# Feed-forward part of a fused convolution and Mamba kernel: the program's order on every engine, a second half put off by a strip, taps in fours

## The chip, the cores and the metric

The kernel runs on one core of one Trainium2 chip. The metric is device time in microseconds (us); the time before is the median of three runs. A profile is one execution recorded by the hardware profiler. TensorE multiplies matrices (PE in the profile, its weight loads PEld), VectorE is DVE, ScalarE is ACT, GpSimd is POOL, and SyncE (SP) issues the transfers.

## The reference, cut to what matters

The input is an image batch of 4 x 64 channels x 128 x 128, float32, and four layers follow one another: a Mamba layer, a mixing layer in a transformed domain, two convolutions with a gate, and a last layer of two convolutions, a Mamba block and a feed-forward block. Only the feed-forward block is touched. With `t` the tokens after the Mamba block:

```
t = t + pvt2ffn(layernorm(t, ln2_w, ln2_b), Hh, Ww, fc1_w, fc1_b, dw_w, dw_b, fc2_w, fc2_b)
y = t.transpose(0, 2, 1).reshape(Bn, C, Hh, Ww)
return x + y

def pvt2ffn(t, Hh, Ww, fc1_w, fc1_b, dw_w, dw_b, fc2_w, fc2_b):
    h = t @ fc1_w.T + fc1_b                       # 64 -> 256 channels
    himg = ...                                    # as an image, 256 x 128 x 128
    himg = conv2d(himg, dw_w, dw_b, groups=Ch)    # 3 x 3, each channel by itself
    h = gelu(himg)                                # back as tokens
    return h @ fc2_w.T + fc2_b                    # 256 -> 64 channels
```

## The kernel before

The kernel is one program of five parts. The last, `layer3_ffn`, reads from device memory the normalised tokens `n3` (`d_n` in the profile) and `s3` (`d_s`), the sum to which its result is added, and writes `out`. It goes through 32 strips: 4 images by 8 strips of R = 16 rows of 128 columns, in a Python loop that is unrolled in full.

The 256 hidden channels are split in two groups of 128. Group 1 (tile `h1`) is convolved on VectorE, group 0 (tile `h0`) on TensorE.

- `first(b, r0, H)` (from line 1409) makes the hidden rows of one strip. It zeroes a border row of the tile `N` at the top strip (L1416) or the bottom strip (L1418) of an image, both on VectorE, loads `N` in two transfers (L1423), and then in six steps, three for `h1` and three for `h0`, multiplies by `f1` into the PSUM tile `ph` (L1436) and lets ScalarE add the bias into `h1` or `h0` (L1441). GpSimd zeroes the border columns (L1427, L1428) and rows (L1430, L1432). It is a generator: the main loop calls it for the strip after, one step after each third tap.
- `taps(h1)` (from line 1454) is VectorE's convolution: one multiplication (L1463) and eight multiply-adds (L1461), each over 16 x 128 elements of 128 channels, into the tile `g1`. It stops after the taps 4 and 8.
- The main loop, for a strip, loads `res` from `s3` in four transfers (L1479). For each half `kk` of the strip (8 rows) it multiplies by nine diagonal matrices, one for each tap, in four 64 x 64 corners of the array, into the PSUM tiles `pd` (L1489), and ScalarE takes the gelu into `g0` (L1499). After the first half comes the gelu of `g1`, in place (L1501).
- Then the first taps of the strip after are called, and after them the output products: for each half `kk`, the PSUM tile `po` gets `f2` times `g1` (L1513) and `f2h` times `g0` (L1516), VectorE adds bias and `res` into `o` (L1520), and after both halves four transfers store `o` (L1524).

`po` and `ph` have one buffer[...], `pd` two buffers[...]. `N`, `h0`, `h1`, `g0`, `g1`, `res` and `o` have two buffers.

The order of the calls is not the order of the instructions: a scheduler of the language takes, for each engine, the instruction that it finds ready and most urgent by its own costs. The two Mamba layers prevent that with a method `pin`, which adds to each new instruction a dependence, without a semaphore, on the one called before it on the same engine. `layer3_ffn` had no such thing.

Of the kernel before, what the change touches and what calls it, by code (L numbers as in the profile page):

```python
# [10 lines left out]
F32 = mybir.dt.float32  # L11
AF = mybir.ActivationFunctionType
ALU = mybir.AluOpType
# [4 lines left out]
P = 128  # L18
B, C, HH, WW = 4, 64, 128, 128
# [94 lines left out]
class _Consts:  # L114


    def __init__(self, nc, pool, cst, upto=None):
        w = _OFF[upto][1] if upto else _CONST.shape[1]
        self.t = pool.tile([P, w], F32, name="cst")
        nc.sync.dma_start(self.t, cst[:, :w])  # L120
# [20 lines left out]

class _Mamba:


# [17 lines left out]
    def __init__(self, ctx, tc, K, nst, w, kinds, bufs, slots={}):  # L164
        nc = self.nc = tc.nc
        self.tc = tc
        self.K, self.nst, self.ng, self.kinds, self.bufs = K, nst, nst // NQ, kinds, bufs
        cp = self.cp = ctx.enter_context(tc.tile_pool(name="mc", bufs=1))
        self.wp = ctx.enter_context(tc.tile_pool(name="mw", bufs=2))
        self.dram = ctx.enter_context(tc.tile_pool(name="md", bufs=2, space=DRAM))  # L170
        self.bp = ctx.enter_context(tc.tile_pool(name="mb", bufs=1, space=PSUM))
        self.misc = ctx.enter_context(tc.tile_pool(name="mm", bufs=1, space=PSUM))
        self.prev, self.seen = {}, None

        self.slots = slots

        wx, xpd, dtw = (self.tmp(k)[:n, :DI] for k, n in (("wx", P), ("xpd", 4), ("dtw", 4)))
        for h in range(2):
            nc.sync.dma_start(wx[64 * h : 64 * (h + 1)], w["in_wT"][:, :DI])
        self.taps = []  # L180
        for k in range(2):
            cw = cp.tile([P, DI], F32, name=f"cw{k}")
            for h in range(2):
                nc.sync.dma_start(
                    cw[64 * h : 64 * (h + 1)],
                    w["conv_wT"][2 * k + h : 2 * k + h + 1, :].to_broadcast([64, DI]),
                )
            nc.vector.tensor_mul(cw, wx, cw)
            self.taps.append(cw)
        self.wz = cp.tile([P, DI], F32, name="wz")  # L190
        nc.vector.memset(self.wz, 0.0)
        nc.sync.dma_start(self.wz[64:], w["in_wT"][:, DI:])
        self.wbc = cp.tile([P, 2 * nst], F32, name="wbc")
        nc.sync.dma_start(self.wbc, w["xp_bcT"])
        self.wC = cp.tile([P, max(nst, DD)], F32, name="wC")
        nc.vector.memset(self.wC, 0.0)
        nc.vector.tensor_copy(self.wC[:, :nst], self.wbc[:, nst:])
        self.spread = {}
        for g in (g for g, kind in enumerate(kinds) if kind == "D"):
            s = self.spread[g] = cp.tile([P, P], F32, name=f"spread{g}")  # L200
            nc.vector.tensor_copy(
                s.rearrange("p (q e) -> p q e", q=NQ),
                self.wbc[:, NQ * g : NQ * (g + 1)].unsqueeze(2).to_broadcast([P, NQ, DD]),
            )

        nc.sync.dma_start(xpd, w["xp_dt"])
        nc.sync.dma_start(dtw, w["dt_wT"])
        pm = self.pm()
        nc.tensor.matmul(pm[:, :DI], xpd, dtw, start=True, stop=True)
        self.wdt = cp.tile([P, DI], F32, name="wdt")  # L210
        nc.vector.tensor_copy(self.wdt, pm[:, :DI])

        cols = {}
        for k in ("conv_b", "dt_b", "D"):
            cols[k] = cp.tile([P, 1], F32, name=f"col_{k}")
            nc.sync.dma_start(cols[k], w[k])
        self.conv_b, self.dt_b, self.z_b = cols["conv_b"], cols["dt_b"], 0.0
        self.dD = cp.tile([P, P], F32, name="dD")
        nc.vector.tensor_scalar(
            self.dD.rearrange("p (j e) -> p j e", j=ND),  # L220
            K.eye.rearrange("p (e j) -> p j e", j=ND),
            cols["D"],
            None,
            ALU.mult,
        )
        self.A = cp.tile([P, ND, self.ng], F32, name="A")
        with nc.allow_non_contiguous_dma(reason="the states on the partitions"):
            for q in range(NQ):
                for j in range(ND):
                    nc.sync.dma_start(  # L230
                        self.A[DD * q : DD * (q + 1), j, :],
                        w["A_log"].rearrange("(e j) (g q) -> j q e g", j=ND, q=NQ)[j, q],
                    )
        nc.scalar.activation(self.A, self.A, AF.Exp)
        nc.vector.tensor_scalar_mul(self.A, self.A, -1.0)
        self.state = cp.tile([P, ND, self.ng], F32, name="state")


        self.ring = cp.tile([P, 2 * ND, GAP + TC], F32, name="ring")
# [28 lines left out]
    def halves(self, *pairs):  # L268
# [5 lines left out]
                for i, (l, r) in enumerate(pairs)  # L274
            )
        )

    def pin(self):

        ins = self.nc.cur_bb.bb.instructions  # L280
        n = len(ins)
        while n and ins[n - 1] is not self.seen:
            n -= 1
        for i in ins[n:]:
            if i.engine in self.prev:
                self.tc.add_manual_dep(
                    i,
                    self.prev[i.engine],
                    mybir.DependencyInfo(mybir.DependencyClass.NoSync, mybir.DependencyReason.DATA),
                    reason="order",  # L290
                )
            self.prev[i.engine] = i.name
        self.seen = ins[-1]

    def t(self, name, bufs=None, w=TC):
        return self.wp.tile([P, w], F32, name=name, tag=name, bufs=bufs)
# [124 lines left out]
    def run(self, chunks, ahead, behind, leads, budget):  # L421
# [3 lines left out]
        nc = self.nc  # L425
# [7 lines left out]
        n = len(its)  # L433
# [15 lines left out]
        owed, full = [], None  # L449
# [65 lines left out]
                    for q in range(NQ):  # L515
                        nc.sync.dma_start(t[DD * q : DD * (q + 1)], rows)

        self.seen = nc.cur_bb.bb.instructions[-1]
        for gen in (ahead, self.prepare):
            for _ in gen(chunks[0]):  # L520
                pass
        replicated(-1)
        produced(0)
        self.pin()
        first, second = {}, {}
        at = -1
        for c in chunks[1:]:
# [4 lines left out]
        for i, (u, j) in enumerate(its):  # L532
# [20 lines left out]
            while nexp < min(n, i + 4) and its[nexp][1] in its[nexp][0]["c"].get("dl", ()):  # L553
                v, k = its[nexp]
# [47 lines left out]
            while owed and not full and (owed[0][0] <= i or i + 1 == n):  # L602
                _, v, h = owed.pop(0)
# [4 lines left out]
                    break  # L608
            beside(i, budget[i % per])
            replicated(i)  # L610
            self.pin()
        for f in list(feeds):
            finished(f)
        finished(started(behind(chunks[-1], self.gated(chunks[-1])), n))
# [747 lines left out]
def layer3_ffn(ctx, tc, K, w, n3, s3, out):  # L1362
# [4 lines left out]
    nc = tc.nc  # L1367
    R = 16
    HR = (R + 2) // 2
    NK = R // 8  # L1370
# [79 lines left out]
    H = {}  # L1450
# [3 lines left out]
    def taps(h1):  # L1454

        g1 = wp.tile([P, R, WW], F32, name="g1", tag="g1")
        for k in range(9):
            dy, dx = divmod(k, 3)
            tap, wk = h1[:, dy : dy + R, dx : dx + WW], dww[:, 1, k : k + 1]
            if k:  # L1460
                nc.vector.scalar_tensor_tensor(g1, tap, wk, g1, ALU.mult, ALU.add)  # L1461
            else:
                nc.vector.tensor_scalar(g1, tap, wk, None, ALU.mult)  # L1463
            if k in (4, 8):
                yield g1

    for g1 in taps(H[1]):
        pass
    for n, (b, r0) in enumerate(strips):
        simg = s3[b].rearrange("c (r w) -> c r w", w=WW)  # L1470
        oimg = out[b].rearrange("c (r w) -> c r w", w=WW)
        h0 = H[0]
        H = {}
        ahead = first(*strips[n + 1], H) if n + 1 < len(strips) else iter(())
# [4 lines left out]
            nc.sync.dma_start(res[half[q % 2], q // 2], simg[:, r0 + 4 * q : r0 + 4 * q + 4, :])  # L1479

        g0 = [wp.tile([P, NK, 4, WW], F32, name=f"g0{i}", tag=f"g0{i}") for i in range(2)]
        for kk in range(NK):
            pd = [dp.tile([P, 4, WW], F32, name=f"pd{i}", tag=f"pd{i}") for i in range(2)]
            for k in range(9):
# [10 lines left out]
                        )  # L1495
                if k % 3 == 2:
                    next(ahead, None)
            for i in range(2):
                nc.scalar.activation(g0[i][:, kk], pd[i], AF.Gelu, bias=dwb[:, i : i + 1])  # L1499
            if not kk:  # L1500
                nc.scalar.activation(g1, g1, AF.Gelu, bias=dwb1)  # L1501
        for _ in ahead:
            pass

        later = taps(H[1]) if H else iter(())
        g2 = next(later, None)

        o = wp.tile([P, NK, 4, WW], F32, name="o3", tag="o3")
        for kk in range(NK):
            po = op.tile([P, 2, 4, WW], F32, name="po", tag="po")  # L1510
            for h in range(2):
                r = 8 * kk + 4 * h
                nc.tensor.matmul(po[half[h], h], f2, g1[:, r : r + 4, :], start=True, stop=False)  # L1513
            for i in range(2):
                for h in range(2):
                    nc.tensor.matmul(  # L1516
                        po[half[h], h], f2h[half[h], i, :], g0[i][half[h], kk], start=False, stop=i == 1
                    )
            for h in range(2):
                nc.vector.scalar_tensor_tensor(  # L1520
                    o[half[h], kk], po[half[h], h], b2[half[h]], res[half[h], kk], ALU.add, ALU.add
                )
        for q in range(R // 4):
            nc.sync.dma_start(oimg[:, r0 + 4 * q : r0 + 4 * q + 4, :], o[half[q % 2], q // 2])  # L1524
        next(later, None)
        g1 = g2


def _col(v):
# [97 lines left out]
```

## Time and profile before

| | |
|---|---|
| median of 3 runs | 19720.83 us (19693.8 to 19727.24) |
| the profiled execution's own time | 19736.35 us |
| its span in the profile | 19734.5 us |
| feed-forward part in it | 18,452 us to the end |
| granted TensorE clock over the span | 0.869 of full speed |

The profile's page gives the busy time of each engine over the whole span and in 40 equal slices; the feed-forward part is a small share of it, so the whole-span shares say little on it. The trace can be asked for windows of time, for the waits in a window (who waited, for whom, total us, times, longest), and for the instructions in order of time. In its lines, `out<-in` names the tiles, `xN` counts instructions run together, and brackets give the idle time before and what ended it. A float32 matrix product shows as two records.

### The profile page before, as it was taken

What the parts mean: (1) busy time and instruction counts of PE and PEld (TensorE: products, weight loads), DVE (VectorE), ACT (ScalarE), POOL (GpSimd) and SP (SyncE); (2) the same over time, 40 slices, a digit from 0 to 9 for tenths busy, and PEclk for the clock granted to TensorE, in tenths of its full rate; (3) what the DMA queues carried; (4) which work ended last, traced back from release to release, by engine and by line L of the source; (5) the groups of instructions that cost most, each with busy time, mean ns of one, the idle gap of its engine ahead of it and who ended that gap; (6) DMA issues with size and microseconds to landing.
All of it is one profiled execution on the core that took longest, in us unless ns stands there. A gap on an engine that the chain in (4) does not pass through costs nothing. (4 is left out here: it accounts for less than half of the span.)

```text
span 19734.5 us, 238606 instructions
## 1 busy us (share of the span) xinstructions
PE 15294.8 (78%) x80186; PEld 7627.5 (39%) x80186; DVE 15836.0 (80%) x8739; ACT 14933.8 (76%) x30369; POOL 14205.9 (72%) x8094
## 2 busy tenths in 40 slices
PE   7778788778897777777777777777777777777777
PEld 3333333367434333333333333333333333333222
DVE  7888888722124999999999999999999999999755
ACT  7888888411324988889888888988889888888422
POOL 6888888500003898899988989998898988989300
PEclk8999899879998888888888888888888888888888
DMA  5555555300212232332323233232322323233111
GB/s 138 152 150 153 154 150 151 95 37 26 75 56 65 75 88 77 84 82 79 87 75 87 78 83 86 76 88 77 83 82 79 87 76 86 78 82 85 46 43 38
DMA packets 669524, 1722.89 MB, mean 87 GB/s; under 512 B 196785, under 2 KB 231937, under 8 KB 660865
## 3 DMA queue, kind: packets, MB, share of 16 engines
q1 hardware_dynamic: 668288, 1707.62, 31.6%
q8 instruction: 629, 10.31, 0.2%
q14 instruction: 607, 4.96, 0.1%
HBM read 1434.27 MB, written 272.63 MB: 86 GB/s over the span
## 5 line engine op out<-in xcount | busy, mean ns | idle before, releaser
L596 POOL TENSOR_TENSOR ring<-ring,cb 128x1024 f32<-128x1024 f32 x5120 | 12086.1, 2378 | 1653.5 <-DVE ring L593 1340.8
L593 DVE TENSOR_TENSOR_SCAN ring<-da,state,bx 128x1024 f32<-128x1024 f32 x4848 | 11143.4, 2335 | 971.1 <-PE bx L494 697.9
L556 ACT ACTIVATE da<-dl,A 128x1024 f32<-128x1024 f32 x5120 | 5868.2, 1146 | 1383.0 <-DVE ring L593 1365.9
L387 ACT ACTIVATE bxT<-duT,BT 128x128 f32<-128x128 f32 x21504 | 6757.2, 387 | 0.0
L494 PE MATMUL bx<-cst,bxT 128*128 128x128 f32 x24576 | 4458.7, 338 | 2842.8 <-DVE bx L587 2053.0
L494 PEld LDWEIGHTS bx<-cst,bxT 128*128 128x128 f32 x24576 | 3743.1, 214 | 4917.0 <-DVE bx L587 2068.7
L413 PE MATMUL y<-ring,cst 128*32 128x512 f32 x20480 | 3566.6, 660 | 332.4 <-POOL ring L596 332.2
L587 DVE TENSOR_TENSOR bx<-du,bx 128x1024 f32<-128x1024 f32 x2048 | 2515.5, 1228 | 339.6 <-PE bx L500 219.1
L413 PEld LDWEIGHTS y<-ring,cst 128*32 128x32 f32 x20480 | 532.3, 112 | 1735.7 <-POOL ring L596 856.1
L1145 PE MATMUL cv<-img,cw 64*64 64x512 f32 x9216 | 1008.2, 594 | 74.6 <-DMA img<-d_x 45.6
L500 PE MATMUL bx<-xc,spread 128*128 128x512 f32 x2048 | 1018.0, 620 | 1.4
L1427 POOL MEMSET h<- 128x18 f32 x64 | 8.3, 132 | 1180.5 <-PE pd L1489 793.5
L1076 POOL TENSOR_TENSOR xs<-xs,cl 128x1024 f32<-128x1024 f32 x32 | 74.9, 2340 | 1068.4 <-DVE cl L1075 1068.4
L391 POOL TENSOR_TENSOR bxT<-duT,BT 128x512 f32<-128x512 f32 x768 | 809.2, 1054 | 11.5 <-ACT duT L370 11.5
L1310 POOL MEMSET X<- 64x1 f32 x4 | 0.4, 89 | 1122.4 <-DMA cw<-in_l_conv_wT 1122.4
L1489 PE MATMUL pd<-h,diag 64*64 64x512 f32 x4608 | 687.9, 610 | 0.7 <-issue 0.7
L1145 PEld LDWEIGHTS cv<-img,cw 64*64 64x64 f32 x9216 | 437.2, 134 | 643.5 <-issue 568.0
L593 DVE TENSOR_TENSOR_SCAN ring<-da,bx 128x1024 f32<-128x1024 f32 x272 | 609.4, 2276 | 72.4 <-PE bx L494 52.8
L500 PEld LDWEIGHTS bx<-xc,spread 128*128 128x128 f32 x2048 | 347.7, 189 | 687.7 <-issue 464.1
L1461 DVE SCALAR_TENSOR_TENSOR g<-h,dww,g 128x2048 f32<-128x2048 f32 x256 | 602.0, 2352 | 11.2
L1441 ACT ACTIVATE h<-ph,ff_fc_b 128x384 f32<-128x384 f32 (+1 forms) x384 | 200.7, 577 | 497.9 <-PE ph L1436 480.1
L1059 ACT COPY O<-p 128x1024 f32<-128x1024 f32 x32 | 32.4, 1012 | 691.7 <-PE p L1052 691.7
(321 smaller groups left out, 13361.0 us busy)
## 6 DMA issues: line engine op xcount, KB each, us to landing
cb<-c SPq DMA_DIRECT2D x5120, 128.0 KB, 2.8
dl<-d SPq DMA_DIRECT2D x2048, 128.0 KB, 3.4
du<-d SPq DMA_DIRECT2D x2048, 128.0 KB, 3.0
d<-pos SPq DMA_DIRECT2D x128, 512.0 KB, 2.6
d<-u SPq DMA_DIRECT2D x128, 512.0 KB, 3.0
X<-d_t SPq DMA_DIRECT2D x124, 256.0 KB, 4.0
S<-in_x SPq DMA_DIRECT2D x120, 256.5 KB, 4.4
res<-in_x SPq DMA_DIRECT2D x128, 128.0 KB, 3.8
```

Source lines behind the costliest of these rows:

```text
L387: nc.scalar.activation(t[:, k, q].rearrange("p e j -> p (e j)"), c["duT"][:, k, :], AF.Copy, scale=c["BT"][:, k, n : n + 1])
L391: nc.gpsimd.tensor_mul(t[:, k].rearrange("p q e j -> p q (e j)"), c["duT"][:, k].unsqueeze(1).to_broadcast(shape), c["BT"][:, k, NQ * g : ...
L413: nc.tensor.matmul(c["y"][DD * j : DD * (j + 1), _COLS[h]], K.sel, hc[:, _COLS[h]], start=False, stop=u["g"] == self.ng - 1,)
L494: nc.tensor.transpose(bx[:, P * k : P * (k + 1)], v["bxT"][:, k, :, :, j].rearrange("p q e -> p (q e)"), self.K.eye)
L500: nc.tensor.matmul(bx[:, k], self.spread[v["g"]], v["c"]["xc"][:, k], start=True, stop=True)
L556: nc.scalar.activation(das[nexp], v["c"]["dl"][k], AF.Exp, scale=self.A[:, k, v["g"] : v["g"] + 1])
L587: nc.vector.tensor_mul(bxs[i], u["c"]["du"][j], u["B"])
L593: nc.vector.tensor_tensor_scan(hs, das.pop(i), bxs.pop(i), 0.0 if u["c"].get("reset") else st, ALU.mult, ALU.add)
L596: nc.gpsimd.tensor_mul(hc, hs, u["cb"])
L1145: nc.tensor.matmul(p[i][half[h]], W[half[i], k, :], src[half[i], at : at + 4, dx : dx + WW], start=k == 0, stop=k == 8,)
L1461: nc.vector.scalar_tensor_tensor(g1, tap, wk, g1, ALU.mult, ALU.add)
L1489: nc.tensor.matmul(pd[i][half[h]], diag[half[i], k, :], h0[half[i], r : r + 4, dx : dx + WW], start=k == 0, stop=k == 8,)
```

## The change

The method `pin` becomes a class of its own, `_Pin`, with the same action; the Mamba layers' loop calls it at the same places. `layer3_ffn` makes one such object before its loop and calls it after each tap and at the end of each half, so that each engine's instructions, the issuing of transfers too, go out in the order of the calls.

The order of the calls changes. The output products of the first half (`kk` = 0) are called in the middle of the second half's taps, after the tap k = 3. Those of the second half are kept in `owed` and called in the next strip, after the tap k = 3 of its first half, with the stores of the strip. VectorE's nine taps are called in three pieces: taps 0 to 3 after the first half and the gelu of `g1`, taps 4 to 7 after the output products of the first half, and tap 8 after the owed half in the next strip. The first strip's nine taps are called ahead of the loop. The last owed half comes after it.

```
+class _Pin:
+    def __init__(self, tc):
+        self.tc, self.prev = tc, {}
+        self.seen = tc.nc.cur_bb.bb.instructions[-1]
+    def __call__(self):
+        ...
...
-            if k in (4, 8):
-                yield g1
+            yield g1
...
+    def more(gen, n):
+        for _ in range(n):
+            g = next(gen, None)
+        return g
+
+    def second(n, g0, g1, res, o, kk):
+        b, r0 = strips[n]
+        po = op.tile([P, 2, 4, WW], F32, name="po", tag="po")
+        ...
+        for h in range(2):
+            nc.vector.scalar_tensor_tensor(
+                o[half[h], kk], po[half[h], h], b2[half[h]], res[half[h], kk], ALU.add, ALU.add
+            )
+        if kk == NK - 1:
+            oimg = out[b].rearrange("c (r w) -> c r w", w=WW)
+            for q in range(R // 4):
+                nc.sync.dma_start(oimg[:, r0 + 4 * q : r0 + 4 * q + 4, :], o[half[q % 2], q // 2])
+
+    pin = _Pin(tc)
+    g1 = more(taps(H[1]), 9)
+    rest, owed = iter(()), None
     for n, (b, r0) in enumerate(strips):
...
         for kk in range(NK):
...
                 if k % 3 == 2:
                     next(ahead, None)
+                if (kk, k) == (0, 3) and owed:
+                    second(*owed)
+                    more(rest, 1)
+                if (kk, k) == (1, 3):
+                    second(n, g0, g1, res, o, 0)
+                    more(rest, 4)
+                pin()
             for i in range(2):
                 nc.scalar.activation(g0[i][:, kk], pd[i], AF.Gelu, bias=dwb[:, i : i + 1])
             if not kk:
                 nc.scalar.activation(g1, g1, AF.Gelu, bias=dwb1)
-        for _ in ahead:
-            pass
-        later = taps(H[1]) if H else iter(())
-        g2 = next(later, None)
...
-        next(later, None)
-        g1 = g2
+                rest = taps(H[1]) if 1 in H else iter(())
+                g2 = more(rest, 4)
+            pin()
+        owed, g1 = (n, g0, g1, res, o, 1), g2
+    second(*owed)
```

More of the change, by code (lines that the diff above doesn't have):

```diff
@@ L138, in _rstd @@
     nc.scalar.activation(out, out, AF.Exp, scale=-0.5)
+class _Pin:
[3 more added lines that the diff above has]
+    def __call__(self):
+        ins = self.tc.nc.cur_bb.bb.instructions
+        n = len(ins)
+        while n and ins[n - 1] is not self.seen:
+            n -= 1
+        for i in ins[n:]:
+            if i.engine in self.prev:
+                self.tc.add_manual_dep(
+                    i,
+                    self.prev[i.engine],
+                    mybir.DependencyInfo(mybir.DependencyClass.NoSync, mybir.DependencyReason.DATA),
+                    reason="order",
+                )
+            self.prev[i.engine] = i.name
+        self.seen = ins[-1]
 class _Mamba:
@@ L172, in __init__ @@
         self.misc = ctx.enter_context(tc.tile_pool(name="mm", bufs=1, space=PSUM))
-        self.prev, self.seen = {}, None
         self.slots = slots
@@ L276, in halves @@
         )
[L278 to L293, printed above, removed]
     def t(self, name, bufs=None, w=TC):
@@ L516, in replicated @@
                         nc.sync.dma_start(t[DD * q : DD * (q + 1)], rows)
-        self.seen = nc.cur_bb.bb.instructions[-1]
+        pin = _Pin(self.tc)
         for gen in (ahead, self.prepare):
@@ L523, in run @@
         produced(0)
-        self.pin()
+        pin()
         first, second = {}, {}
@@ L610, in run @@
             replicated(i)
-            self.pin()
+            pin()
         for f in list(feeds):
@@ L1463, in taps @@
                 nc.vector.tensor_scalar(g1, tap, wk, None, ALU.mult)
-            if k in (4, 8):
-                yield g1
-    for g1 in taps(H[1]):
-        pass
+            yield g1
[7 more added lines that the diff above has]
+        for h in range(2):
+            r = 8 * kk + 4 * h
+            nc.tensor.matmul(po[half[h], h], f2, g1[:, r : r + 4, :], start=True, stop=False)
+        for i in range(2):
+            for h in range(2):
+                nc.tensor.matmul(po[half[h], h], f2h[half[h], i, :], g0[i][half[h], kk], start=False, stop=i == 1)
+        for h in range(2):
+            nc.vector.scalar_tensor_tensor(
+                o[half[h], kk], po[half[h], h], b2[half[h]], res[half[h], kk], ALU.add, ALU.add
+            )
+        if kk == NK - 1:
[5 more added lines that the diff above has]
+    rest, owed = iter(()), None
     for n, (b, r0) in enumerate(strips):
         simg = s3[b].rearrange("c (r w) -> c r w", w=WW)
-        oimg = out[b].rearrange("c (r w) -> c r w", w=WW)
         h0 = H[0]
@@ L1481, in layer3_ffn @@
         g0 = [wp.tile([P, NK, 4, WW], F32, name=f"g0{i}", tag=f"g0{i}") for i in range(2)]
+        o = wp.tile([P, NK, 4, WW], F32, name="o3", tag="o3")
         for kk in range(NK):
@@ L1497, in layer3_ffn @@
                     next(ahead, None)
+                if (kk, k) == (0, 3) and owed:
[4 more added lines that the diff above has]
+                    more(rest, 4)
+                pin()
             for i in range(2):
@@ L1501, in layer3_ffn @@
                 nc.scalar.activation(g1, g1, AF.Gelu, bias=dwb1)
-        for _ in ahead:
-            pass
-        later = taps(H[1]) if H else iter(())
-        g2 = next(later, None)
[L1508 to L1524, printed above, removed]
-        next(later, None)
-        g1 = g2
+                rest = taps(H[1]) if 1 in H else iter(())
+                g2 = more(rest, 4)
+            pin()
+        owed, g1 = (n, g0, g1, res, o, 1), g2
+    second(*owed)
 def _col(v):
```

## The prediction

> **What bounds the kernel now.** I went from the table of busy time by slices (the feed-forward part is the last 2.6 of its 40 slices) to the busy time by windows, the waits of that stage and the timeline of single strips. Everything outside this part keeps its instructions and their order: the pinning moved from a method to a class, and the two Mamba layers call it at the same places. So only the time from 18,452 us to the end is in question.
>
> The windows, columns as named in the second line: two windows, one of about a strip and, for later, one of a convolution stage.
>
> ```profile
> core 0: us, PE busy (x) PEld busy (x) DVE busy (x) ACT busy (x) POOL busy (x), PEclk, DMA share, GB/s
> 5400.00:5700.00 300.00, 300.00 (x2800) 104.72 (x2796) 47.98 (x64) 67.71 (x92) 0.00 (x0) 1.00 0.15 50
> ...
> 19111.40:19151.20 39.80, 30.64 (x192) 9.03 (x192) 23.10 (x13) 10.64 (x17) 0.35 (x4) 0.84 0.16 42
> ```
>
> In 39.8 us TensorE is busy 30.6, VectorE 23.1, ScalarE 10.6: no engine is full. The waits of the stage (18,490 us to the end; total us, times, longest) say why:
>
> ```profile
> DVE g L1463 <- ACT h L1441: 321.9, 31, 10.8
> ...
> ACT g L1501 <- DVE g L1461: 299.9, 30, 10.9
> PE po L1513 <- DVE o L1520: 288.1, 32, 10.1
> ...
> DVE o L1520 <- PE po L1516: 177.5, 33, 16.8
> ```
>
> TensorE loses 9.0 us a strip to VectorE's addition (L1520), and VectorE loses 10.4 to `h` and 5.4 to TensorE: the two stand in each other's way in turn. The timeline (start, duration) shows it in one strip:
>
> ```profile
> 19130.75 1.28 DVE L1463 TENSOR_SCALAR g<-h,dww 128x2048 f32<-128x2048 f32 x1 [10.59 <-ACT h L1441]
> ...
> 19131.83 0.92 PE L1436 MATMUL ph<-N,f 64*128 64x384 f32 x4
> 19132.07 19.13 DVE L1461 SCALAR_TENSOR_TENSOR g<-h,dww,g 128x2048 f32<-128x2048 f32 x8
> ...
> 19135.42 0.92 PE L1436 MATMUL ph<-N,f 64*128 64x384 f32 x4
> ...
> 19139.85 1.08 PE L1513 MATMUL po<-g,f 128*64 128x512 f32 x4
> ...
> 19151.24 1.53 DVE L1520 SCALAR_TENSOR_TENSOR o<-po,fc2b__124169,res 64x512 f32<-64x512 f32 x2
> 19151.30 2.00 ACT L1501 ACTIVATE g<-g,dwb 128x2048 f32<-128x2048 f32 x1 [9.97 <-DVE g L1461]
> ...
> 19152.82 1.97 PE L1513 MATMUL po<-g,f 128*64 128x512 f32 x4 [9.18 <-DVE o L1520]
> ```
>
> All nine taps of the next strip run in one piece, 19,130.75 to 19,151.2. The first half's products are in `po` by 19,143, but the addition that frees the single `po` is queued behind the taps; the second half's products stand at the head of TensorE's queue until 19,152.82. The additions of halves 0 are at 18,522.44 for strip 0 and 19,700.82 for strip 30: 39.28 us a strip.
>
> [...]after the 9.18 us wait the first L1513 group took 1.97 us instead of 1.08. [...]here, with one core, the window at 5,400 us shows 300 of 300 us busy at clock 1.00.[...]
>
> **The change part by part.** I write t for the time in a strip, from its first `pd` product.
>
> *TensorE, the sum.* Three taps of `pd` and one `ph` group come every 3.58 us at full clock (19,131.83 to 19,135.42); six of these are 21.5. One `po` half is 12 matmul records: 1.0 for the four of L1513, four steps of 0.43 for the eight of L1516, 2.75; two are 5.5. Sum 27.0 with no stall. Nothing is added or removed; the order is.[...]
>
> *The path through one strip.* k0-2 0 to 2.6, `ph` to 3.6, k3 to 4.4, owed `po` half to 7.3, then k4-8 with two `ph` groups: kk=0 ends at 13.6. Its gelus are needed late: those of the strip before end by 2.4, `po` wants them at 4.4. ScalarE after kk=0: `h` 13.8 to 14.9 (1.07 after the `ph` start, 1.05 long), two `pd` gelus to 16.15, gelu of `g1` (2.00) to 18.2. TensorE in kk=1: k0-2 and `ph` to 17.15, k3 to 18.0, then `second(n, 0)`, which needs `g1` at 18.2: a new wait, 0.2 to 0.5. I take 0.3: **27.3 us a strip**, from 26.8 (a cheaper `po`, no wait) to 28.5[...]. The half clock goes with the 9 us stall.
>
> *VectorE, in its own order.* Taps 0-3 (1.32 + 3 x 2.39 = 8.5) start when `h1` is complete, 14.9, end 23.4; addition of half 0, whose `po` is ready at 21.1, to 24.9; taps 4-7 (9.6) to 34.5, which is 7.2 of the next strip; addition of the owed half, `po` ready 7.3, to 8.8; tap 8 to 11.2. Behind the additions wait taps 4-7 and tap 8; the gelu of `g1` wants tap 8 at 16.15, so 5 us are spare. Busy 23.4 of 27.3, waiting 3.7: VectorE doesn't bound. `po` is free at 8.8 and 24.9, wanted at 18 and at 31.7.
>
> *Image starts.* `first` issues VectorE's zeroing of the top row of `N` (L1416, 0.17 us) at the strip's start, in program order now behind tap 7, so done at 7.4; the `ph` at t=2.7 of strips 7, 15 and 23 reads that row. TensorE waits 4.7[...]. Three times 6.2 is 18.6 us (0 to 30). The bottom row (L1418) is read only by the third group, at 12.8: hidden. Loads of `N` don't wait for it: they were issued at 18,707.7, the zeroing ran at 18,718.9.
>
> *SP, POOL.* The four stores of a strip (0.47 each to issue) come after the owed addition, at 8.8 to 10.7 of the next strip, past the two loads of `N` and four of `res`, which are now issued ahead of them and, for the strip after, behind them: ten issues, some 5.5 of 27.3 us. `N` for the strip after goes out by 12 and lands 4.3 later, wanted at 30; `res` is wanted at 21 of the next strip. Cost zero; with that slack of 14 us gone, TensorE would wait for `ph`. POOL does four small memsets a strip (0.13 each); their tiles are free half a strip before ScalarE writes them: zero. All tiles that live longer have two buffers. Bytes per strip are the same in less time: 42 x 39.28/27.3 = 60 GB/s, and the page shows slices of 150.
>
> *The sum.* Strip 0 depends on the same chain as now (first `h`, nine taps until 18,497.5); its `pd` ended at 18,510.2, and with one `po` half in between strip 1 starts at 18,512.9. Thirty strips of 27.3 are 819, image starts 18.6. Strip 31 has no `ph`: 15.5 + 2.75 + the wait to 21.4, gelus and the last half to 25, addition 1.53: 26.4; from the last addition to the end 3.2, as now. 18,512.9 + 819 + 18.6 + 29.6 = 19,380, 354 below the span of 19,734.5. The profiled execution took 19,736.35, which gives 19,382; the median of the runs is 15.5 lower, so **19,366**.
>
> **Rivals.** (1) *VectorE becomes the bound*: its order now alternates with TensorE, and if the 5.4 us for `po` of today stay beside 23.4 busy and 1.7 for `h`, a strip is 30.5 us: 30 x 3.2 = 96 more, 19,462. For it: taps 4-7 end within 0.1 us of the owed `po`. Against: each `po` is ready when VectorE comes. Chance 0.11.
>
> (2) *Slower: the array stays at half clock.*[...] 27.0 us of products become 54, 14.7 more than 39.28: 30 x 14.7 = 441, 20,162. It decides below a mean clock of 27.0/39.28 = 0.69. For it: the clock of this stage is 0.84 to 0.89 now[...]. Against: clock 1.00 in the full convolution window. Chance 0.06.
>
> (3) *The change doesn't do what it says*: the order is still that of today, nine taps in front of the addition. Then 19,721. For it: the call order was a wish before as well, and was not kept. Against: the same pinning sets the Mamba layers' order. Chance 0.03.
>
> **How the numbers follow.** The forecast, TensorE-bound at 26.8 to 28.5 us, has 0.80. Its bottom: 15 for 26.8 and 19 for free image starts, with 22 for the scatter of runs (the lowest is 27 below the median): 19,310. Its top: 36 for 28.5 and 11 for the image starts, some 19,415. I widen the range to 19,470 to take in rival 1. What a measurement of this kernel can tell from no change is about 0.2%, 39 us. The first two cases are faster (0.91), the third is the same (0.03), the second rival slower (0.06).
>
> **What would show it.** Right: additions of halves 0 at 27.3 us steps, TensorE's wait for L1520 near nothing, clock near 1.00, VectorE waiting 3 to 4 us before the first tap, a small wait of `po` for the gelu of `g1`, and three longer waits of `ph` at image starts behind L1416. Wrong: a strip over 28.5 us, or a wait of TensorE over 1 us in an ordinary strip; the name of who ends it tells which step failed.

## The result, and the profile after

The changed kernel took 19,395.9 us (median of four runs, 19,381.6 to 19,397.5) against 19,722.3 before: 0.9836 of it, 95% interval 0.9819 to 0.9853, or 326 us less. The forecast was 19,366 within 19,310 to 19,470.

In the two profiled executions the feed-forward part, from the addition into its bias (L1397, now L1403) to the end, took 1270.9 us before (18,463.59 to 19,734.5) and 939.6 us after (18,453.95 to 19,393.5): 331 us less. It began 9.6 us earlier in the second one. The layers ahead are unchanged, but in the ten profiled executions of this document they end anywhere between 18,413 and 18,466 us. That scatter is as large as some of the differences below, so the strip and the time from that addition to the end (the stage time) are compared beside the totals.

The busy time in a window of exactly one strip of the changed kernel:

```profile
core 0: us, PE busy (x) PEld busy (x) DVE busy (x) ACT busy (x) POOL busy (x), PEclk, DMA share, GB/s
18936.60:18964.58 27.98, 27.98 (x194) 8.63 (x193) 23.03 (x14) 10.40 (x17) 0.35 (x4) 1.00 0.25 59
```

A strip takes 27.98 us where it took 39.28. TensorE is shown busy without a gap, at a granted clock of 1.00; before, it was busy 30.6 of 39.8 us at 0.84. The waits of the stage, 18,490 us to the end (who waited for whom: total us, times, longest):

```profile
DVE g L1469 <- ACT h L1447: 104.1, 31, 3.4
DVE o L1488 <- PE po L1486: 63.8, 32, 7.9
...
PE ph L1442 <- DVE N L1422: 12.7, 3, 4.5
...
PE po L1483 <- ACT g L1540: 1.0, 1, 1.0
```

The 288 us that TensorE spent waiting for VectorE's addition are gone from the list. VectorE waits 3.4 us a strip for `h` and some 1 us for `po`. The three waits of `ph` for the zeroed border row are there. The first of them:

```profile
18679.71 1.65 PE L1442 MATMUL ph<-N,f 64*128 64x384 f32 x4 [4.11 <-DVE N L1422]
```

The group after the wait takes 1.65 us, at a granted clock of 0.50, where it takes 0.92 in an ordinary strip, at 1.00.

One strip in order of time (start, us), with the addition of each half in its new place:

```profile
18935.76 0.92 PE L1442 MATMUL ph<-N,f 64*128 64x384 f32 x4
...
18936.60 3.54 PE L1521 MATMUL pd<-h,diag 64*64 64x512 f32 x24
18936.72 1.05 ACT L1447 ACTIVATE h<-ph,ff_fc_b 128x384 f32<-128x384 f32 x2 [2.53 <-PE ph L1442]
...
18937.35 0.30 PEld L1521 LDWEIGHTS pd<-h,diag 64*64 64x64 f32 x8 [0.56 <-ACT h L1447]
...
18941.94 1.08 PE L1483 MATMUL po<-g,f 128*64 128x512 f32 x4
...
18944.93 1.53 DVE L1488 SCALAR_TENSOR_TENSOR o<-po,fc2b__124169,res 64x512 f32<-64x512 f32 x2 [1.12 <-PE po L1486]
...
18952.24 1.29 DVE L1469 TENSOR_SCALAR g<-h,dww 128x2048 f32<-128x2048 f32 x1 [3.39 <-ACT h L1447]
...
18953.16 2.02 ACT L1540 ACTIVATE g<-g,dwb 128x2048 f32<-128x2048 f32 x1
...
18955.56 1.08 PE L1483 MATMUL po<-g,f 128*64 128x512 f32 x4
...
18960.79 1.53 DVE L1488 SCALAR_TENSOR_TENSOR o<-po,fc2b__124169,res 64x512 f32<-64x512 f32 x2
```

Two things are to be seen. The owed half (18,941.94) gets its addition as soon as its products are there. And the first 24 `pd` records of the strip take 3.54 us, where such a group takes 2.81 elsewhere: the weights of the tap's second product (its lower four rows) wait until 18,937.35 for ScalarE. This wait doesn't show as idle time of TensorE, since the first product, in the other two corners of the array, was still running: its four records go from 18,936.60 to 18,937.67.

### The profile page after: what moved, and what is told of

It is laid out like the page before. It is cut to its first block, busy times and chain, and to the rows that moved or that the text cites. A ratio compares the mean times of both kernels' runs of the same rounds, so it can differ in the third digit from the quotient of the medians.

```text
span 19393.5 us, 238514 instructions
## 1 busy us (share of the span) xinstructions
PE 15226.3 (79%) x80186; PEld 7611.8 (39%) x80186; DVE 15837.4 (82%) x8739; ACT 14924.4 (77%) x30369; POOL 14204.5 (73%) x8094
## 5 line engine op out<-in xcount | busy, mean ns | idle before, releaser
L1521 PE MATMUL pd<-h,diag 64*64 64x512 f32 x4608 | 632.1, 603 | 0.7 <-issue 0.7
```

The costliest lines, as they stand in the source:

```text
L1521: nc.tensor.matmul(pd[i][half[h]], diag[half[i], k, :], h0[half[i], r : r + 4, dx : dx + WW], start=k == 0, stop=k == 8,)
```

## The experiments

Theory A was: a strip is bound by TensorE; the 0.7 us above the forecast are `h0`'s last rows, three image starts cost what the queue behind tap 7 costs, and the gain comes from taking the addition out from behind nine taps. Each rival (theory B) is named in the expectation it belongs to.

**Hidden rows one tap earlier.** In the changed kernel:

```
-                if k % 3 == 2:
+                if k % 3 == 1:
                     next(ahead, None)
```

> The changed kernel, with each of the six steps that make the next strip's hidden rows called one tap earlier (after k = 1, 4, 7 instead of 2, 5, 8). Theory A: the 0.73 us that each strip loses at its start is TensorE's second pd product waiting for the last rows of h0, which ScalarE writes 1.5 us after their ph product; one tap of 0.86 us between them covers it, so a strip goes from 27.98 to 27.25 us, 22 us in all; the three image starts wait 0.86 longer each; total near 19,376. Theory B: the 0.73 us belongs to the change of tile shapes around ph and pd and comes along: 27.98 stays, total 19,396 to 19,400.

Measured: 19,373.3 us (0.9823 of before, 0.9808 to 0.9837), stage 918.0 us. The first taps stand 27.24 us apart in an ordinary strip, as theory A has it. The strip's start in its timeline:

```profile
18931.38 0.92 PE L1442 MATMUL ph<-N,f 64*128 64x384 f32 x4
...
18932.23 2.81 PE L1521 MATMUL pd<-h,diag 64*64 64x512 f32 x24
```

These 24 records are the last tap of a strip and the first two of the next, and take 2.81 us again. ScalarE's rows are now covered by a tap. So 0.74 us of the 27.98 were the wait for `h0`, and theory B falls: the tile shapes change as often as before, and the 0.74 us are gone.

**Border row on GpSimd.** In the changed kernel, twice:

```
-            nc.vector.memset(N[:64, 0:1, :], 0.0)
+            nc.gpsimd.memset(N[:64, 0:1, :], 0.0)
```

> The changed kernel, with the border row of N zeroed on GpSimd instead of VectorE. Theory A: the three long strips at image starts (35.0, 33.8 us and a third, against 27.98) come from the zeroing queued behind tap 7; on GpSimd it is done at once, these strips become 27.98, 19 us less, total near 19,377, VectorE's order else unchanged. Theory B: ph then waits for the load of N or for GpSimd's own queue, and the strips stay above 30 us: total 19,385 to 19,396.

The second edit does the same to the bottom row. Measured: 19,377.7 us (0.9827, 0.9813 to 0.9842), as theory A has it; stage 919.3 us. The steps between first taps at the image starts are 28.06 instead of 35.01, 33.83 and 35.38 us. `ph` is no longer in the list of waits of TensorE; GpSimd itself waits 0.3 us for the tile:

```profile
POOL N L1422 <- PE ph L1442: 0.9, 3, 0.3
```

Three zeroings of 0.17 us each cost 20 us in all for their place in a queue alone.

**Pinning alone.** The kernel before, its own order of calls, with a `_Pin` called after each tap, each half and each strip.

```
+    pin = _Pin(tc)
     for g1 in taps(H[1]):
         pass
...
                 if k % 3 == 2:
                     next(ahead, None)
+                pin()
...
         next(later, None)
+        pin()
         g1 = g2
```

> The kernel before with the pinning alone: its own order of calls (both halves of the output products at the strip's end, taps 0 to 4 ahead of them and 5 to 8 after), held on every engine. Theory A: what cost 9 us was the addition behind nine taps, and holding any order with the addition between taps takes it away; TensorE then waits 1.6 us for the first half's addition between the halves: 21.5 + 2 x 2.87 + 1.6 = 28.9 us a strip, image starts some 9 to 11 us each, total near 19,440. Theory B: the gain needs the second half moved into the next strip and the taps in fours; without them most of the 9 us stays: over 36 us a strip, total over 19,640.

Measured: 19,625.7 us (0.9952, 0.9936 to 0.9969), stage 1177.8 us; 36.1 us in an ordinary strip on the mean (34.8 to 37.4), 40.3 to 40.4 at the image starts. Theory A's numbers were missed by far. Theory B's strip of over 36 us was met and its total missed by 14 us, but the cause is neither theory's: a wait that both had missed. In the list of waits (18,560 to 19,600 us) it is a load:

```profile
PE ph L1460 <- DMA N<-d_n: 94.4, 40, 3.9
...
PE po L1540 <- DVE o L1547: 47.4, 29, 1.6
PE ph L1460 <- DVE N L1440: 26.6, 3, 8.9
```

The 1.6 us for the addition between the halves are as expected. The timeline shows the rest:

```profile
19075.97 5.84 SPq L1551 DMA_DIRECT2D out<-o  x4
...
19076.79 1.08 PE L1540 MATMUL po<-g,f 128*64 128x512 f32 x4 [1.64 <-DVE o L1547]
...
19081.90 1.19 SPq L1447 DMA_DIRECT2D N<-d_n  x2
...
19085.72 0.91 PE L1460 MATMUL ph<-N,f 64*128 64x384 f32 x2 [3.41 <-DMA N<-d_n]
...
19088.04 4.18 PE L1514 MATMUL pd<-h,diag 64*64 64x512 f32 x24
```

SyncE holds the last stores until the second addition, at the strip's end; the load of `N` for the strip after is called behind them, goes out at 19,081.9, and TensorE is ready for it at 19,082.3 (19,085.72 less the wait). After the wait of 3.41 us the next 24 `pd` records take 4.18 us instead of 2.81: from 19,088.95 to 19,090.66 their weight loads are 0.86 us apart, in the group that starts at 19,093.00 they are 0.43.

**The same with SyncE's queue free.**

```
         for i in ins[n:]:
+            if i.engine == mybir.EngineType.SP:
+                continue
```

> The kernel before with the pinning alone, as in the earlier experiment of that kind, but with SyncE's queue left to the scheduler, which in the built program puts the loads of N ahead of the stores again. Theory A: the 36.4 us a strip there, against the 28.9 expected, come from N loaded behind the stores that wait for the second addition, 3.7 us of wait and the half clock after it; with SP free a strip is 28.9 to 30 us and the total 19,430 to 19,480. Theory B: the half clock and the wait come from the two halves at the strip's end themselves: over 34 us a strip, total over 19,580.

Measured: 19,427.3 us (0.9849, 0.9835 to 0.9864), stage 985.4 us, 28.78 us in an ordinary strip: just below theory A's figures, and far from theory B's. Two first taps, and the waits (18,560 to 19,300 us):

```profile
18518.52 1.29 DVE L1489 TENSOR_SCALAR g<-h,dww 128x2048 f32<-128x2048 f32 x1 [0.67 <-ACT h L1467]
...
18547.30 1.28 DVE L1489 TENSOR_SCALAR g<-h,dww 128x2048 f32<-128x2048 f32 x1 [0.67 <-ACT h L1467]
```

```profile
PE po L1542 <- DVE o L1549: 40.9, 25, 1.6
PE ph L1462 <- issue: 26.6, 3, 8.9
```

The wait for the load is gone, the one between the halves stands, and the image starts are 39.5 to 40.4 us, dearer than in the changed kernel. The second row gives their wait to "issue", the same three times and 8.9 us that the run before put down to the zeroing of `N`. So program order on the compute engines, without any new place for the calls, brings the strip from 39.28 to 28.78 us.

**New call places, no pinning.** The changed kernel without its `pin()` calls in `layer3_ffn`.

```
-    pin = _Pin(tc)
...
-                pin()
...
-            pin()
```

> The changed kernel without its pinning: the new places of the calls, the order left to the scheduler. In the built program VectorE's queue still has an addition after five taps and another after four more, and TensorE's has no half behind nine taps. Theory A: the new call places alone bring the gain: 27.2 to 28.5 us a strip, total 19,355 to 19,415. Theory B (the prediction's third rival in a weaker form): the scheduler's order makes TensorE wait again by several us a strip: 31 us or more, total over 19,490.

Measured: 19,804.7 us (1.0044, 1.0029 to 1.0059), slower than before by a little more than the noise; stage 1348.2 us, 41.8 us a strip. Theory A falls. Theory B holds, with a strip 11 us beyond its lower bound. The wait is not for VectorE's addition:

```profile
19007.14 1.26 ACT L1536 ACTIVATE g<-pd,dwb 128x512 f32<-128x512 f32 x2 [1.69 <-PE pd L1520]
...
19017.95 2.00 ACT L1538 ACTIVATE g<-g,dwb 128x2048 f32<-128x2048 f32 x1 [9.54 <-DVE g L1467]
19019.85 1.03 ACT L1447 ACTIVATE h<-ph,ff_fc_b 128x384 f32<-128x384 f32 x2
...
19020.47 1.13 PE L1520 MATMUL pd<-h,diag 64*64 64x512 f32 x4 [10.52 <-ACT h L1447]
```

ScalarE's queue holds the gelu of `g1`, which waits 9.54 us for the last tap, in front of the last rows of `h0`, whose `ph` ended at 19,007.9. TensorE waits 10.52 us for those rows in every strip.

**Only ScalarE pinned.** The changed kernel, where `_Pin` passes over all engines but one.

```
+            if self.only is not None and i.engine != self.only:
+                continue
...
-    pin = _Pin(tc)
+    pin = _Pin(tc, mybir.EngineType.Activation)
```

> The changed kernel with only ScalarE pinned, the other queues left to the scheduler. Theory A: the 41.8 us a strip without any pinning came from ScalarE's queue, where the gelu of g1, waiting for the last tap, had been put in front of the last rows of h0 that TensorE needs (10.5 us a strip); with ScalarE in the order of the calls that wait goes and TensorE waits only 2 to 4 us for the gelus, since the scheduler has put each po half after the first tap instead of the fourth: 30 to 33 us a strip, total 19,470 to 19,560. Theory B: the order on TensorE and VectorE carries the gain, and without it a strip stays at 38 us or more: total over 19,700.

Measured: 19,372.2 us (0.9817, 0.9803 to 0.9832), stage 919.4 us. That is less than either theory had. Theory A's wait of 2 to 4 us didn't come: in this run each `po` half stands where the calls put it, after the tap k = 3, and not after the first tap. The first taps of two strips:

```profile
18992.48 1.29 DVE L1471 TENSOR_SCALAR g<-h,dww 128x2048 f32<-128x2048 f32 x1 [4.41 <-ACT h L1449]
...
19020.46 1.29 DVE L1471 TENSOR_SCALAR g<-h,dww 128x2048 f32<-128x2048 f32 x1 [4.40 <-ACT h L1449]
```

They are 27.98 us apart, as with all engines pinned, and the image starts are 28.09: the scheduler set the zeroing early enough by itself. With the new call places, holding ScalarE's order is enough, and costs 20 us less in the stage than holding every engine's. Whether it would be enough with the call places of before was not tried.

**Nine taps in one piece.** In the changed kernel:

```
-                    more(rest, 1)
...
-                    more(rest, 4)
...
-                g2 = more(rest, 4)
+                g2 = more(rest, 9)
```

> The changed kernel with VectorE's nine taps in one piece after the first half instead of 4, 4 and 1; all else as changed, pinned. Theory A: the nine taps (20.45 us from 15.6 us of the strip on) hold back the first half's addition to 37.6; the owed half, due on TensorE at 33.2, waits 4.5 us for po in every strip: 32.5 us a strip, up to 34.5 if the wait brings half clock; total 19,535 to 19,600. Theory B: the taps' division is of no account since VectorE has 3.7 us to spare a strip: 28 to 28.5 us, total under 19,415.

Measured: 19,560.1 us (0.9919, 0.9903 to 0.9936), stage 1122.0 us; 33.9 to 34.7 us in an ordinary strip: at the upper end of theory A's, with the total inside its range. The waits (18,560 to 19,300 us) have the old one back at half its size:

```profile
PE po L1483 <- DVE o L1488: 77.5, 18, 4.3
```

and slow groups after it:

```profile
18991.20 1.97 PE L1483 MATMUL po<-g,f 128*64 128x512 f32 x4 [4.25 <-DVE o L1488]
```

1.97 us against 1.08 for the same four records, and the L1486 records behind them follow at steps of 0.86 us (18,994.01, 18,994.87) where the changed kernel has 0.43 (18,943.43, 18,943.86). The mean granted clock from 18,452 to 19,340 us was 0.92, in the changed kernel 0.97. Of the 6.2 us more a strip, 4.3 are the wait and about 1.9 are left for the slow groups after it.

**Both mends together.** The edits of the first two experiments.

> The changed kernel with both mends, the hidden rows' steps one tap earlier and N's border row zeroed on GpSimd. If the two shortfalls are independent, as theory A has it, they add: 27.24 us in every strip, image starts too, TensorE waiting nowhere over 0.3 us; 22 + 21 us below the changed kernel's 19,396, so 19,350 to 19,357. If one had hidden the other, the total stays at 19,370 or above.

Measured: 19,348.1 us (19,343.0 to 19,351.1), 0.9808 of before (0.9793 to 0.9822), and 48 us under the changed kernel, just below the range expected. A window of one strip:

```profile
18936.60:18963.84 27.24, 27.24 (x196) 8.24 (x192) 23.10 (x14) 10.59 (x18) 0.36 (x4) 1.00 0.26 61
```

Every step between first taps, image starts too, is 27.16 to 27.32 us, apart from the first two. The two shortfalls add: the stage takes 895.5 us, 44.0 less than in the changed kernel, where the two edits alone took off 21.5 and 20.3. This is the best version that was run.

## Why the prediction was right, and where its sizes were off

*What bounds the kernel.* Right: the strip went from two engines waiting in turn to TensorE at a granted clock of 1.00. The nine-taps run shows VectorE's division to be needed (6.2 us a strip), and the slow clock went with the wait: in the strip of the kernel before that the prediction shows, the granted clock fell to 0.50 at 19,145.8, in the wait of 9.18 us, and was 1.00 again from 19,156.1; over the stage it was 0.87 before and is 0.99 now.

*The sum for a strip.* 27.3 was forecast, 27.98 measured: over thirty strips, 20 of the 23 us by which the stage was missed. The 28.5 at the top of the forecast was the author's estimate. The terms: the six groups are 3.58 each, as taken. A `po` half costs 2.87 (the step from `ph` to `ph` around it is 6.45, 18,953.70 to 18,960.15) and not 2.75: 0.24 for both. The small wait for the gelu of `g1`, put at 0.3, isn't there: the gelu ends at 18,955.18, `po` starts at 18,955.56. These two errors nearly cancel, which is luck. The step that failed is the one that was left out: the first tap's second product reads rows 4 to 7 of `h0`, and the last of the six hidden-row steps writes rows 6 to 8 and 15 to 17 just ahead of it: 0.73 us a strip that the sum put at nothing. The kernel before had the same dependence, with a `po` half between the two; moving that half to after k = 3 took the cover away. The prediction costed each thing that the moved half now waits for, and not what it had been hiding where it stood.

*Image starts.* 6.2 us each were forecast, 7.0, 5.9 and 7.4 measured; mechanism and place as stated. The wait was a little shorter than the 4.7 taken (4.1, 4.1 and 4.5), and the slow stretch after it dearer than the 1.5 that 6.2 leaves for it, which was the author's estimate: 2.9, 1.7 and 2.9 us were lost there. In these stretches TensorE worked for 5.9, 3.4 and 6.0 us at a granted clock of 0.50.

*SP at no cost.* Right in the changed kernel, and the pinning-alone run shows the price if the slack is gone: stores called at the strip's end in front of the load cost 36.1 - 28.8 = 7.3 us in an ordinary strip, a wait of 3.7 and slow groups after it. In the changed kernel a strip's last stores are called in the next strip, behind the load of `N`, which in its pinned queue then goes out well ahead of its use: at 18,947.05 for the `ph` at 18,968.06.

*The rivals.* VectorE never became the bound: it is busy 23.03 of 27.98 us. The granted clock was 1.00 in the ordinary strip shown; only the three waits at image starts were followed by slow groups. The second rival, a low clock through the whole stage, was the author's estimate; the stage's mean is 0.99. The third rival held that the order would stay that of before; the timeline shows the additions between the taps. Without pinning the time is worse than before, by a wait on ScalarE's queue that no step of the prediction had named.

*What the parts are worth.* Against 39.28 us a strip: order on the compute engines alone, SyncE left to the scheduler, 28.78; with SyncE pinned too, the second half moved and the taps in fours 27.98; new places without any held order 41.8. So most of the gain is from the order kept: 286 of the 331 us of the stage come without any new call place. In an ordinary strip the new places take away the wait of 1.6 us between the halves and bring in the 0.73 us for `h0`, so they are worth 0.8 there, besides cheaper image starts and what they do for SyncE.

What stays open is why the scheduler, with the new calls and no pinning, puts the gelu of `g1` ahead of the rows of `h0`; what it reckoned with is not in the traces. Open too is whether pinning ScalarE alone would be enough with the old call places.

## What to carry to other kernels

When work is moved out of a gap, ask what that work was hiding where it stood, not only what it will wait for where it goes. In a queue kept in program order, go through every engine's list for the small things, a zeroing, a store, a load, that now stand behind something long: they cost what they wait, not what they take (here three zeroings of 0.17 us cost 20 us). Where an order left to a scheduler leaves engines waiting for each other in turn, try the order of the calls, and find out which single queue needs it.

## What was not expected of the hardware

A wait of 4.3 us and one of 3.4 us were each followed by slow TensorE groups: four L1483 records in 1.97 us for 1.08, and 24 `pd` records in 4.18 us for 2.81. The wait of 1.6 us between the halves wasn't: the four records after it took 1.08. What the slow stretch cost was not fixed by the wait: after waits of 4.11 and 4.12 us at two image starts, 2.9 and 1.7 us were lost beyond the wait. The granted clock was 0.50 from 18,678.9 to 18,685.6 us in the first case, and from 18,911.0 to 18,914.3 in the second, where it was still 1.00 when the wait ended at 18,910.51. And a wait of half of the array showed in the trace as a long group (3.54 for 2.81 us), not as an idle TensorE; a window that reads 27.98 of 27.98 us busy still held 0.74 us to be had.
